# Edge-count products of a graph network on one core: four-pass fp32 against a one-pass format with split operands

## The chip, the core and the metric

The kernel runs on one NeuronCore of one Trainium2 chip. The metric is the device time of one execution in microseconds; several executions are taken and the median counts. Three runs of the kernel before took 2294.43, 2296.43 and 2296.47 us, a median of 2296.43 us.

The engines are called as the profile calls them: PE is TensorE, which multiplies matrices (PEld is its weight load), DVE is VectorE, ACT is ScalarE, POOL is GpSimd, and SP is SyncE, which issues most of the large DMAs. PE writes to PSUM only; DVE and ACT move its results on to SBUF.

## What is computed

The reference runs two blocks of a graph transformer over 625 nodes of 1024 features and 10000 edges. The change lies in the second block's graph part, a two-layer mean-aggregating network, which stands between a linear attention and an attention with experts:

```python
xn = _layernorm(x)
deg_inv = 1 / maximum(segment_sum(ones, dst), 1)
def layer(h, W_self, W_neigh, b):
    agg = segment_sum(h[src], dst)          # sum over incoming edges
    return h @ W_self + (agg * deg_inv[:, None]) @ W_neigh + b
h = relu(layer(xn, W_self0, W_neigh0, b0))
x = x + layer(h, W_self1, W_neigh1, b1) + linear_attention(xn) @ Wo.T + bo
```

With a matrix C whose entry (src, dst) is the number of edges from src to dst, the aggregation is a product: C transposed times h. The kernel builds C once, from one-hot vectors of the edges, and uses it as the operand `CT`.

## The kernel before, in words

The 625 nodes are cut into five tiles (`NT = 5`) of 125 rows (`P`), and the 1024 features into eight chunks (`KC`) of 128 or two column halves of 512. Arrays that end in `T` have features on partitions and nodes along the row, padded to 626 columns (`NP`), which a product takes in two halves of 313 (`HN`). Weights stream from HBM through a pool of six buffers of 1 MB (`wpool`); a `Half` is one column half of a weight matrix and takes two of them. SP issues their DMAs in program order, each when its buffer is free.

In the part from the first edge to the second block's attention, PE, DVE, ACT, POOL and SP run in exactly the order in which the code is written (a hand-made schedule). A small class `Stream` (`do`) arranges it: each call `do(prep, pe, after, after2)` first emits the evictions (`after`) that earlier calls left over, and then its own matmuls (`pe`). So the eviction of a product stands behind whatever DVE work the code wrote between the two calls.

What the change and the steps of the prediction touch, in the order in which it runs:

- `count` and `decode` (L413, L434) build `CT`, an fp32 tile of shape 125 x 5 x 626, for the first block's attention. It then holds integers.
- `degrees` (L985) takes the self loops out of `CT`, multiplies it with a matrix of ones (`pdeg`), and inverts the sums: `dinv`, one number for each column, the same on all partitions. L1010 and L1011 then multiply `CT` by `dinv`, while PE computes keys and values of the linear attention.
- The linear attention's last loop runs over eight chunks `m`. `query(m+1)` computes `pq`, from which ACT makes `qe` and `qf` (L305, L307) and DVE finishes `qf` (L308). `answer(m)` computes `pd` and `po`, and DVE makes `z` and the result `oT` (L324, L325, L326). `qe` and `z` share one buffer; `pq`, `pd` and `po` take turns in three PSUM buffers of two banks (`ps2`). For `m` = 0 and 1, DVE also writes `xnh` (L1025) here, the normalised rows of one column half, five tiles of 125 x 512 each. It stands behind `answer(m)`'s matmuls and ahead of its eviction.
- `pa` (L1039): for each of the eight chunks, `xnh` times `CT`, ten matmuls of 313 columns, copied alternately by DVE and ACT to `meanT`.
- `ph`: the first layer's two weight products, ending in `hT`.
- `pz`: `hT` times `W_neigh1`, copied to `z`, for both column halves, one after the other.
- `last_of(t, c)` (L1125): for tile `t` and column half `c` one PSUM group of 8 matmuls of `hT` with `W_self1`, 8 of `oT` with `Wo` and 5 of `CT` with `z`, each of 512 columns; DVE adds the sum to `x` (L1134). The loop takes `c` = 0 and 1 of a tile, one after the other, with `norm_rows(t-1)` (row statistics on DVE and ACT) between them and `turn_rows(t-1)` (eight transposes `ptr` of the normalised rows and two DVE evictions into `nxT`, L1086) behind them. `px` and `ptr` share two one-bank PSUM buffers (`ps1`).
- `keys`, `q0` and `value` begin the next attention from `nxT`; the first, `keys[0](0)`, reads its columns 0 to 312, so tiles 0 to 2.

Of the kernel before, what the change touches and what calls it, by code (L numbers as in the profile page):

```python
# [8 lines left out]
FP = mybir.dt.float32  # L9
BF = mybir.dt.bfloat16  # L10
HF = mybir.dt.float16
I32 = mybir.dt.int32
AF = mybir.ActivationFunctionType
ALU = mybir.AluOpType
# [4 lines left out]
N = 625  # L19
NT = 5  # L20
# [18 lines left out]


def gps_kernel(tc: tile.TileContext, w: dict, out: bass.AP):


    again = attempt(tc, w, out, False)
    with tc.If(again > 0):
        attempt(tc, w, out, True)
# [3 lines left out]
def attempt(ctx: ExitStack, tc: tile.TileContext, w: dict, out: bass.AP, shifted: bool):  # L50
# [8 lines left out]
    def ps1(name):  # L59
        pool, n = psums[-1]  # L60
        return pool.tile([128, 512], FP, tag="ps1", name=name, bufs=n)
# [33 lines left out]
    def copy(dst, src):  # L95

        turn[0] ^= 1
        if turn[0]:
            nc.vector.tensor_copy(dst, src)
        else:  # L100
            nc.scalar.activation(dst, src, AF.Copy)  # L101
# [21 lines left out]
    def group(dst, pairs):  # L123

        for i, (lhsT, rhs) in enumerate(pairs):
            nc.tensor.matmul(dst, lhsT=lhsT, rhs=rhs, start=(i == 0), stop=(i == len(pairs) - 1))  # L126

    def feat(name, pairs):

        p = ps2(name)  # L130
        for h in range(2):
            group(p[:, h, :HN], [(a, b[:, h * HN:(h + 1) * HN]) for a, b in pairs])
        return p[:, :, :HN]

    def halves(ap):
        return ap.rearrange("p (h n) -> p h n", h=2)

    def nodes(t):
        return slice(t * P, (t + 1) * P)
# [23 lines left out]

    graph = ctx.enter_context(ExitStack())
    gpool = graph.enter_context(tc.tile_pool(name="graph", bufs=1))
    CT = gpool.tile([P, NT, NP], FP, tag="CT", name="CT")
    xrows = w["x"].rearrange("(t p) d -> t p d", p=P)

    class Stream:
# [35 lines left out]
    def mid(shape, name):  # L205
        return midp.tile(shape, FP, tag="mid", name=name)
# [124 lines left out]
    with ExitStack() as st0:  # L331
# [9 lines left out]
        with ExitStack() as edges:  # L341
# [71 lines left out]
            def count():  # L413

                if part["held"] or part["done"] == EN:
                    return False
                lo, hi, t = counting[part["done"]]
                part["held"] = 2 * (t == hi - 1)

                def prep():  # L420
                    while len(made_ahead) < min(8, EN - t):
                        one_hot()
                    hold["hot"] = made_ahead.pop(0)
                    part["done"] += 1

                def pe():
                    od, os = hold["hot"]
                    if t == lo:
                        part["pc"] = psums[-1][0].tile([128, NT, 512], FP, tag="pct", name="pct", bufs=1)
                    for j in range(NT):  # L430
                        nc.tensor.matmul(part["pc"][:P, j, :HN], lhsT=os[:, nodes(j)],
                                         rhs=od[:, :HN], start=(t == lo), stop=(t == hi - 1))

                def decode():  # L434
                    for j in range(0, NT, 2):
                        js = slice(j, min(j + 2, NT))
                        n = js.stop - j
                        low, high, v = CT[:, js, 0:HN], CT[:, js, HN:NP], part["pc"][:P, js, :HN]
                        u = pool.tile([P, 2, HN], FP, tag="u", name="u", bufs=1)[:, 0:n, :]

                        nc.vector.tensor_scalar(u, v, 1728.0, BIG, op0=ALU.subtract, op1=ALU.add)
                        nc.vector.tensor_scalar(u, u, BIG, None, op0=ALU.subtract)
                        if lo == 0:
                            nc.vector.tensor_tensor(low, v, u, op=ALU.subtract)
                            nc.vector.tensor_scalar(high, u, 1.0 / 4096, None, op0=ALU.mult)
                        else:
                            nc.vector.scalar_tensor_tensor(high, u, 1.0 / 4096, high, op0=ALU.mult, op1=ALU.add)
                            nc.vector.tensor_tensor(u, v, u, op=ALU.subtract)
                            nc.vector.tensor_tensor(low, low, u, op=ALU.add)
                    if hi == EN:  # L450

                        for s in range(NT):
                            nc.vector.tensor_tensor(CT[:, s, nodes(s)], CT[:, s, nodes(s)], ident[:P, :P],
                                                    op=ALU.add)

                do(prep, pe, decode if t == hi - 1 else None)
                return True
# [519 lines left out]
        do.flush()  # L977

    dinv = mix.tile([P, NP], FP, tag="qe", name="dinv", bufs=1)
    b0_t = mix.tile([128, KC], FP, tag="bq", name="b0_t", bufs=2)
    nc.gpsimd.dma_start(out=b0_t, in_=w["b0"])

    def degrees():  # L985
        for t in range(NT):
            nc.vector.tensor_tensor(CT[:, t, nodes(t)], CT[:, t, nodes(t)], ident[:P, :P], op=ALU.subtract)

        def pe():
            pdeg = hold["pdeg"] = ps2("pdeg")  # L990
            for h in range(2):
                group(pdeg[:P, h, :HN], [(ones[:P, :P], CT[:, s, h * HN:(h + 1) * HN]) for s in range(NT)])

        def after():
            nc.vector.tensor_scalar(halves(dinv), hold["pdeg"][:P, :, :HN], 1.0, None, op0=ALU.max)
            nc.vector.reciprocal(dinv, dinv)

        do(None, pe, after)

    states = [lin1.states()]  # L1000
    lin1.half(1)
# [5 lines left out]
    for t in range(1, NT):  # L1007
        lin1.key(t)
        lin1.value(t)
        nc.vector.tensor_tensor(CT[:, t, :], CT[:, t, :], dinv, op=ALU.mult)  # L1010
    nc.vector.tensor_tensor(CT[:, 0, :], CT[:, 0, :], dinv, op=ALU.mult)  # L1011
    oT = bigT("oT1")
    lin1.query(0)
    for f in lin1.states():
# [2 lines left out]
    for m in range(KC):  # L1017
        if m + 1 < KC:
            lin1.query(m + 1)
        lin1.answer(m, oT)  # L1020
        if m < 2:

            xh = mid([P, NT, 512], "xnh")
            for t in range(NT):
                nc.vector.tensor_scalar(xh[:, t, :], x[:, t, m * 512:(m + 1) * 512], mv1[:, t, 0:1],  # L1025
                                        rs1[:, t:t + 1], op0=ALU.subtract, op1=ALU.mult)
            xnh.append(xh)
    for name in ("b1", "L1_bo"):
        b_t = mix.tile([128, D], FP, tag="kv", name="b_t", bufs=2)
        nc.gpsimd.dma_start(out=b_t, in_=w[name].to_broadcast([128, D]))  # L1030
# [3 lines left out]
    for k in range(KC):  # L1034
        if k % 4 == 0:
            meanT.append(mid([128, 4, NP], "meanT"))

        def pe():
            hold["pa"] = feat("pa", [(xnh[k // 4][:, s, k % 4 * 128:k % 4 * 128 + 128], CT[:, s, :])  # L1039
                                     for s in range(NT)])  # L1040

        def after(k=k):
            copy(halves(meanT[k // 4][:, k % 4, :]), hold["pa"])

        do(None, pe, after)
    hT = []
    for m in range(KC):
# [10 lines left out]
            nc.scalar.activation(halves(hT[m // 4][:, m % 4, :]), hold["ph"], AF.Relu, bias=b0_t[:, m:m + 1])  # L1058

        do(None, pe, after)  # L1060
    z = big.tile([P, NT, D], FP, tag="big", name="z")
    for c in range(2):
        wn1 = Half(wpool, w["W_neigh1"], c)
        for t in range(NT):
            def pe():
                hold["pz"] = ps1("pz")
                group(hold["pz"][:P], [(hT[k // 4][:, k % 4, nodes(t)], wn1(k)) for k in range(KC)])

            def after(t=t, c=c):
                copy(z[:, t, c * 512:(c + 1) * 512], hold["pz"][:P])  # L1070

            do(None, pe, after)
    ws = [Half(wpool, w["W_self1"], c) for c in range(2)]
    wo = [Half(wpool, w["L1_Wo"], 0), Half(midp, w["L1_Wo"], 1, tag="mid", padded=[128, 4, 645])]
    mixed_up.close()


    rows_d = dram.tile([N + 1, D], FP, name="rows_d")
    y_d = dram.tile([128 * NB, D], FP, name="y_d")
    few = ctx.enter_context(tc.tile_pool(name="few", bufs=1, reuse_waits="tile"))  # L1080
    attn = ctx.enter_context(ExitStack())
    pool = attn.enter_context(tc.tile_pool(name="attn", bufs=1, reuse_waits="tile"))

# [40 lines left out]

    def last_of(t, c):  # L1125
        def pe():
            hold["px"] = ps1("px3")
            group(hold["px"][:P], [(hT[k // 4][:, k % 4, nodes(t)], ws[c](k)) for k in range(KC)]
                  + [(oT[:, k, nodes(t)], wo[c](k)) for k in range(KC)]
                  + [(CT[:, s, nodes(t)], z[:, s, c * 512:(c + 1) * 512]) for s in range(NT)])  # L1130

        def after():
            xc = x[:, t, c * 512:(c + 1) * 512]
            nc.vector.tensor_tensor(xc, hold["px"][:P], xc, op=ALU.add)  # L1134

        do(None, pe, after)

    for t in range(NT):
        last_of(t, 0)
        if t:  # L1140
            norm_rows(t - 1)
        last_of(t, 1)
        if t:
            turn_rows(nxT, t - 1, 0)


    kvc = mid([128, 2 * NP + NT * 256], "kvc")
# [36 lines left out]
                      kcT[:, a, :]) for a in range(2)]  # L1184
    q0 = [query(0, a) for a in range(2)]
    keys[0](0)
    norm_rows(NT - 1)
    keys[1](0)
    q0[0](0)
# [515 lines left out]
```

## Time and profile before

| | us |
|---|---|
| median of three runs | 2296.43 |
| the profiled execution's own time | 2290.41 |
| its span, first to last instruction | 2288.7 |
| POOL's L1032, ten additions to x beside the answers' loop | 24.4 |
| DVE's two copies of `z` and `meanT` (L99), x5 and x4 | 3.5, 3.2 |
| ACT's two copies of `z` and `meanT` (L101), x5 and x4 | 3.0, 2.8 |
| DVE's `CT` by `dinv` (L1010, L1011), x5 | 4.0 |
| `pdeg`, x20 | 5.4 |

The page gives for each group of instructions the line, engine and operation, the tile written and those read, the shapes, the count, the busy time, the mean nanoseconds of one, and the idle time of the engine ahead of it with what ended it. The busy time of a group is the union of its intervals. A PE record is longer than the pace of the instructions, since matmuls overlap: the pace is read from start to start. Each fp32 matmul of the code appears as two MATMUL records with a weight load each: the 80 products of `pa` in the code are x160 in the profile, the 50 products of `CT` with `z` are x100. A bf16 matmul appears once.

The mean granted clock of TensorE over the span is 0.978 of full speed.

### The profile page before, as it was taken

How to read it: one execution, taken by the hardware profiler on the slowest of the kernel's cores; microseconds unless marked ns; L12 is line 12 of the kernel's file. 1: busy time of each engine (PE TensorE's matmuls, PEld its weight loads, DVE VectorE, ACT ScalarE, POOL GpSimd, SP SyncE). 2: the span in 40 equal slices, each digit the busy share in tenths (PEclk: the TensorE clock that was granted, in tenths of full speed). 3: DMA queues.
4: the chain of work that ended last, by engine and by line, in shares of the span. 5: the costliest groups of instructions: out<-in, count | busy, mean ns of one | idle time of the engine just before them, and what ended most of it. 6: DMA issues, size and time to landing. Idle time of an engine off the chain costs nothing. (4 is left out here: it accounts for less than half of the span.)

```text
span 2288.7 us, 17693 instructions
## 1 busy us (share of the span) xinstructions
PE 2170.3 (95%) x7018; PEld 1228.9 (54%) x7018; DVE 734.7 (32%) x1342; ACT 196.1 (9%) x363; POOL 346.0 (15%) x351
## 2 busy tenths in 40 slices
PE   8988888987899999999999999999999999999998
PEld 6655554444445767754444777556754444444443
DVE  5868668655422640000111133232111111111112
ACT  2000010012200100000000011110000000000000
POOL 1667766300000220010000000010000000000010
PEclk9998998989999999999999999999999999999999
DMA  9352252530122110233003111030269898898643
GB/s 302 96 174 63 68 186 79 133 105 1 37 83 74 46 46 0 74 138 110 0 0 118 57 38 37 10 109 1 92 249 338 318 332 305 303 332 319 254 149 94
DMA packets 145852, 301.66 MB, mean 132 GB/s; under 512 B 12370, under 2 KB 22436, under 8 KB 145754
## 3 DMA queue, kind: packets, MB, share of 16 engines
q1 hardware_dynamic: 123412, 243.18, 29.6%
q0 software_dynamic: 17664, 47.47, 7.0%
q10 hardware_dynamic: 4678, 9.72, 1.4%
q8 instruction: 59, 0.97, 0.2%
q14 instruction: 39, 0.32, 0.0%
HBM read 277.49 MB, written 22.84 MB: 131 GB/s over the span
## 5 line engine op out<-in xcount | busy, mean ns | idle before, releaser
L126 PE MATMUL pu<-w,xgT 128*128 128x512 f32 x768 | 333.9, 593 | 1.9 <-DVE xgT L1086 1.9
L126 PEld LDWEIGHTS pu<-w,xgT 128*128 128x128 f32 x768 | 144.0, 190 | 174.8 <-issue 172.0
L126 PE MATMUL pyb<-w,hb 128*128 128x512 f32 x384 | 174.3, 598 | 2.5 <-ACT yb L101 2.1
L126 PE MATMUL pq<-xnT,w 128*128 128x313 f32 x512 | 143.0, 439 | 15.1 <-ACT qf L307 11.6
L126 PE MATMUL pv<-w,xnT 128*125 128x512 f32 x320 | 143.4, 602 | 3.7 <-issue 3.7
L126 PE MATMUL pk<-w,xnT 128*125 128x512 f32 x320 | 141.4, 595 | 4.7 <-DVE x L888 4.7
L126 PE MATMUL p<-tT,w 128*128 128x313 f32 x512 | 136.3, 428 | 0.4 <-DVE tT L1086 0.4
L126 PEld LDWEIGHTS pq<-xnT,w 128*128 128x128 f32 x512 | 99.6, 196 | 56.9 <-ACT qf L307 13.5
L126 PEld LDWEIGHTS pyb<-w,hb 128*128 128x128 f32 x384 | 69.8, 189 | 90.9 <-issue 74.9
L1539 DVE TENSOR_TENSOR su<-pu,su 128x512 f32<-128x512 f32 x24 | 16.6, 691 | 314.6 <-ACT su L1538 314.6
L126 PEld LDWEIGHTS p<-tT,w 128*128 128x128 f32 x512 | 96.8, 190 | 37.9 <-issue 1.2
L126 PEld LDWEIGHTS pk<-w,xnT 128*125 128x125 f32 x320 | 59.7, 189 | 78.9 <-issue 72.2
L126 PEld LDWEIGHTS pv<-w,xnT 128*125 128x125 f32 x320 | 60.4, 191 | 76.7 <-issue 75.9
L582 POOL DMA_INDIRECT table<-es,at x79 | 85.9, 1088 | 59.9 <-issue 27.2
L1522 POOL DMA_INDIRECT xg<-rows_d,slots x12 | 11.4, 947 | 524.7 <-PE pxg L1529 449.0
L568 POOL DMA_INDIRECT ga<-xl_d,si x79 | 81.1, 1027 | 32.1 <-issue 29.1
L568 POOL DMA_INDIRECT gb<-xr_d,di x79 | 79.6, 1008 | 24.1 <-issue 23.5
L706 PE MATMUL px<-w,oT 128*125 128x512 f32 x160 | 76.7, 639 | 4.1 <-DVE oT L326 2.3
L126 PE MATMUL px<-w,hT 128*125 128x512 f32 x160 | 70.6, 594 | 0.0
L126 PE MATMUL px<-w,oT 128*125 128x512 f32 x160 | 70.3, 592 | 0.0
L126 PE MATMUL ph<-meanT,w 128*128 128x313 f32 x256 | 70.1, 426 | 0.0
L126 PE MATMUL ph<-xnT,w 128*128 128x313 f32 x256 | 70.0, 427 | 0.0
(352 smaller groups left out, 2550.9 us busy)
## 6 DMA issues: line engine op xcount, KB each, us to landing
w<-in_eW_dram SPq DMA_DIRECT2D x144, 1024.0 KB
w<-in_L_Wk_dram SPq DMA_DIRECT2D x8, 1024.0 KB
w<-in_L_Wv_dram SPq DMA_DIRECT2D x8, 1024.0 KB
w<-in_L_Wq_dram SPq DMA_DIRECT2D x8, 1024.0 KB
w<-in_L_Wo_dram SPq DMA_DIRECT2D x8, 1024.0 KB
w<-in_W_self_dram SPq DMA_DIRECT2D x8, 1024.0 KB
w<-in_W_neigh_dram SPq DMA_DIRECT2D x8, 1024.0 KB
w<-in_sW_dram SPq DMA_DIRECT2D x8, 1024.0 KB
```

The lines of the kernel that those rows point to most:

```text
L126: nc.tensor.matmul(dst, lhsT=lhsT, rhs=rhs, start=(i == 0), stop=(i == len(pairs) - 1))
L568: nc.gpsimd.indirect_dma_start(out=dst[0:p, j, :], out_offset=None, in_=src[:, :], in_offset=bass.IndirectOffsetOnAxis(ap=ix[0:p, lo + j:l ...
L582: nc.gpsimd.indirect_dma_start(out=table[:, :], out_offset=bass.IndirectOffsetOnAxis(ap=at[0:p, lo + j:lo + j + 1], axis=0), in_=es[0:p, l ...
L706: nc.tensor.matmul(hold["px", t][:P, c, :], lhsT=oT[:, k, nodes(t)], rhs=wo[c](k), start=(k == 0), stop=False)
L1522: nc.gpsimd.indirect_dma_start(out=xg, out_offset=None, in_=rows_d[:, :], in_offset=bass.IndirectOffsetOnAxis(ap=slots[:, b:b + 1], axis=0))
L1539: nc.vector.tensor_tensor(su, pu[:, 0, :], su, op=ALU.mult)
```

## The change

`CT` becomes a tile of the type float32r (`FR`), a 4-byte format of reduced precision that TensorE is to take in one pass; its whole edge counts are written in it. Where other code reads it, it is seen as fp32 through a bitcast. `CT` is no longer multiplied by `dinv`; the degrees are applied to the results instead. The other operand of each product, which isn't made of small integers, is split into a high part (an ACT copy rounded to the format) and a low part (DVE: the value less the high part), and both are multiplied with `CT` into the same sum. The last products are taken by column halves: all five tiles of the first half, then `z` and the weights of the second half, then its tiles. (The path `shifted` is a second attempt with full fp32 and isn't run for these inputs.)

```diff
-    CT = gpool.tile([P, NT, NP], FP, tag="CT", name="CT")
+    CTr = gpool.tile([P, NT, NP], FP if shifted else FR, tag="CT", name="CT")
+    CT = CTr if shifted else CTr.bitcast(FP)
...
     def degrees():
...
         def after():
-            nc.vector.tensor_scalar(halves(dinv), hold["pdeg"][:P, :, :HN], 1.0, None, op0=ALU.max)
+            nc.vector.tensor_scalar(halves(dinv), hold["pdeg"][:, :, :HN], 1.0, None, op0=ALU.max)
+            if not shifted:
+                most = sage.tile([128, 1], FP, name="most")
+                nc.vector.tensor_reduce(most, dinv, AX.X, ALU.max)
+                nc.vector.tensor_scalar(inside[:, 1:2], most, 4095.0, None, op0=ALU.is_le)
             nc.vector.reciprocal(dinv, dinv)
+            own = mix.tile([P, NP], FP, tag="qe", name="own", bufs=1)[:, 0:N].rearrange("p (t n) -> p t n", t=NT)
+            nc.vector.tensor_tensor(own, dinv[:P, 0:N].rearrange("p (t n) -> p t n", t=NT),
+                                    ident[:P, :P].unsqueeze(1).to_broadcast([P, NT, P]), op=ALU.mult)
+            nc.vector.tensor_reduce(dinvT, own, AX.X, ALU.add)
...
+    def split(src, high, low):
+        nc.scalar.activation(high, src, AF.Copy)
+        if not shifted:
+            nc.vector.tensor_tensor(low, src, high.bitcast(FP), op=ALU.subtract)
...
     for t in range(1, NT):
         lin1.key(t)
         lin1.value(t)
-        nc.vector.tensor_tensor(CT[:, t, :], CT[:, t, :], dinv, op=ALU.mult)
-    nc.vector.tensor_tensor(CT[:, 0, :], CT[:, 0, :], dinv, op=ALU.mult)
...
         lin1.answer(m, oT)
         if m < 2:
-            xh = mid([P, NT, 512], "xnh")
+            parts = [midp.tile([P, NT, 512], NUM, tag="mid", name="xnh")]
+            parts.append(sage.tile([P, NT, 512], NUM, name="xnl") if m else
+                         midp.tile([P, NT, 512], NUM, tag="mid", name="xnl"))
             for t in range(NT):
-                nc.vector.tensor_scalar(xh[:, t, :], x[:, t, m * 512:(m + 1) * 512], mv1[:, t, 0:1],
+                xh = mix.tile([P, 512], FP, tag=("kb", "ke")[t % 2], name="xh", bufs=1)
+                nc.vector.tensor_scalar(xh, x[:, t, m * 512:(m + 1) * 512], mv1[:, t, 0:1],
                                         rs1[:, t:t + 1], op0=ALU.subtract, op1=ALU.mult)
-            xnh.append(xh)
+                split(xh, parts[0][:, t, :], parts[1][:, t, :])
+            xnh.append(parts[0:1] if shifted else parts)
...
         def pe():
-            hold["pa"] = feat("pa", [(xnh[k // 4][:, s, k % 4 * 128:k % 4 * 128 + 128], CT[:, s, :])
-                                     for s in range(NT)])
+            p = hold["pa"] = ps2("pa")
+            for h in range(2):
+                group(p[:, h, 0:HN + 1], [(xp[:, s, k % 4 * 128:k % 4 * 128 + 128],
+                                           CTr[:, s, h * (HN - 1):h * (HN - 1) + HN + 1])
+                                          for xp in xnh[k // 4] for s in range(NT)])
 
         def after(k=k):
-            copy(halves(meanT[k // 4][:, k % 4, :]), hold["pa"])
+            m = meanT[k // 4][:, k % 4, :]
+            for h in range(2):
+                nc.vector.tensor_tensor(m[:, h * HN:(h + 1) * HN], hold["pa"][:, h, h:h + HN],
+                                        dinv[:, h * HN:(h + 1) * HN], op=ALU.mult)
...
-    z = big.tile([P, NT, D], FP, tag="big", name="z")
-    for c in range(2):
+    z, ws, wo = [], [], []
+    def neighbours(c):
+        zc = big.tile([P, 2, NT, 512], NUM, tag="big", name="z")
+        z.append(zc)
         wn1 = Half(wpool, w["W_neigh1"], c)
+        ws.append(Half(wpool, w["W_self1"], c))
+        wo.append(Half(wpool, w["L1_Wo"], c))
         for t in range(NT):
...
-            def after(t=t, c=c):
-                copy(z[:, t, c * 512:(c + 1) * 512], hold["pz"][:P])
+            def after(t=t):
+                split(hold["pz"][:P], zc[:, 0, t, :], zc[:, 1, t, :])
...
-    ws = [Half(wpool, w["W_self1"], c) for c in range(2)]
-    wo = [Half(wpool, w["L1_Wo"], 0), Half(midp, w["L1_Wo"], 1, tag="mid", padded=[128, 4, 645])]
+    neighbours(0)
...
     def last_of(t, c):
         def pe():
-            hold["px"] = ps1("px3")
-            group(hold["px"][:P], [(hT[k // 4][:, k % 4, nodes(t)], ws[c](k)) for k in range(KC)]
-                  + [(oT[:, k, nodes(t)], wo[c](k)) for k in range(KC)]
-                  + [(CT[:, s, nodes(t)], z[:, s, c * 512:(c + 1) * 512]) for s in range(NT)])
+            p = hold["px"] = ps2("px3")
+            group(p[:P, 0, :], [(hT[k // 4][:, k % 4, nodes(t)], ws[c](k)) for k in range(KC)]
+                  + [(oT[:, k, nodes(t)], wo[c](k)) for k in range(KC)])
+            group(p[:P, 1, :], [(CTr[:, s, nodes(t)], z[c][:, i, s, :]) for i in range(1 if shifted else 2)
+                                for s in range(NT)])
 
         def after():
             xc = x[:, t, c * 512:(c + 1) * 512]
-            nc.vector.tensor_tensor(xc, hold["px"][:P], xc, op=ALU.add)
+            nc.vector.tensor_tensor(xc, hold["px"][:P, 0, :], xc, op=ALU.add)
+            nc.vector.scalar_tensor_tensor(xc, hold["px"][:P, 1, :], dinvT[:, t:t + 1], xc,
+                                           op0=ALU.mult, op1=ALU.add)
...
     for t in range(NT):
         last_of(t, 0)
+    neighbours(1)
+    for t in range(NT):
+        last_of(t, 1)
         if t:
             norm_rows(t - 1)
-        last_of(t, 1)
-        if t:
-            turn_rows(nxT, t - 1, 0)
+        if t > 1:
+            turn_rows(nxT, t - 2, 0)
...
     keys[0](0)
+    turn_rows(nxT, NT - 2, 0)
     norm_rows(NT - 1)
```

The small pool `few` moves to the other end of SBUF; `pdeg` has 128 instead of 125 stationary columns; `dinvT` is a column of five inverse degrees for each partition.

More of the change, by code (lines that the diff above doesn't have):

```diff
@@ L11 @@
 HF = mybir.dt.float16
+FR = mybir.dt.float32r
 I32 = mybir.dt.int32
@@ L438, in decode @@
                         low, high, v = CT[:, js, 0:HN], CT[:, js, HN:NP], part["pc"][:P, js, :HN]
+                        low_r, high_r = CTr[:, js, 0:HN], CTr[:, js, HN:NP]
                         u = pool.tile([P, 2, HN], FP, tag="u", name="u", bufs=1)[:, 0:n, :]
@@ L443, in decode @@
                         if lo == 0:
-                            nc.vector.tensor_tensor(low, v, u, op=ALU.subtract)
-                            nc.vector.tensor_scalar(high, u, 1.0 / 4096, None, op0=ALU.mult)
+                            nc.vector.tensor_tensor(low_r, v, u, op=ALU.subtract)
+                            nc.vector.tensor_scalar(high_r, u, 1.0 / 4096, None, op0=ALU.mult)
                         else:
-                            nc.vector.scalar_tensor_tensor(high, u, 1.0 / 4096, high, op0=ALU.mult, op1=ALU.add)
+                            nc.vector.scalar_tensor_tensor(high_r, u, 1.0 / 4096, high, op0=ALU.mult, op1=ALU.add)
                             nc.vector.tensor_tensor(u, v, u, op=ALU.subtract)
-                            nc.vector.tensor_tensor(low, low, u, op=ALU.add)
+                            nc.vector.tensor_tensor(low_r, low, u, op=ALU.add)
                     if hi == EN:
                         for s in range(NT):
-                            nc.vector.tensor_tensor(CT[:, s, nodes(s)], CT[:, s, nodes(s)], ident[:P, :P],
+                            nc.vector.tensor_tensor(CTr[:, s, nodes(s)], CT[:, s, nodes(s)], ident[:P, :P],
                                                     op=ALU.add)
@@ L977, in attempt @@
         do.flush()
-    dinv = mix.tile([P, NP], FP, tag="qe", name="dinv", bufs=1)
+    few = ctx.enter_context(tc.tile_pool(name="few", bufs=1, side="right", reuse_waits="tile"))
+    sage = mixed_up.enter_context(tc.tile_pool(name="sage", bufs=1, reuse_waits="tile"))
+    dinv = sage.tile([128, NP], FP, name="dinv")
+    dinvT = few.tile([P, NT], FP, name="dinvT")
     b0_t = mix.tile([128, KC], FP, tag="bq", name="b0_t", bufs=2)
@@ L986, in degrees @@
         for t in range(NT):
-            nc.vector.tensor_tensor(CT[:, t, nodes(t)], CT[:, t, nodes(t)], ident[:P, :P], op=ALU.subtract)
+            nc.vector.tensor_tensor(CTr[:, t, nodes(t)], CT[:, t, nodes(t)], ident[:P, :P], op=ALU.subtract)
         def pe():
@@ L991, in pe @@
             for h in range(2):
-                group(pdeg[:P, h, :HN], [(ones[:P, :P], CT[:, s, h * HN:(h + 1) * HN]) for s in range(NT)])
+                group(pdeg[:, h, :HN], [(ones[:P, :], CT[:, s, h * HN:(h + 1) * HN]) for s in range(NT)])
         def after():
-            nc.vector.tensor_scalar(halves(dinv), hold["pdeg"][:P, :, :HN], 1.0, None, op0=ALU.max)
+            nc.vector.tensor_scalar(halves(dinv), hold["pdeg"][:, :, :HN], 1.0, None, op0=ALU.max)
[3 more added lines that the diff above has]
+                nc.vector.tensor_scalar(inside[:, 1:2], most, 4095.0, None, op0=ALU.is_le)
             nc.vector.reciprocal(dinv, dinv)
+            own = mix.tile([P, NP], FP, tag="qe", name="own", bufs=1)[:, 0:N].rearrange("p (t n) -> p t n", t=NT)
+            nc.vector.tensor_tensor(own, dinv[:P, 0:N].rearrange("p (t n) -> p t n", t=NT),
+                                    ident[:P, :P].unsqueeze(1).to_broadcast([P, NT, P]), op=ALU.mult)
+            nc.vector.tensor_reduce(dinvT, own, AX.X, ALU.add)
         do(None, pe, after)
+    def split(src, high, low):
+        nc.scalar.activation(high, src, AF.Copy)
+        if not shifted:
+            nc.vector.tensor_tensor(low, src, high.bitcast(FP), op=ALU.subtract)
+    NUM = FP if shifted else FR
     states = [lin1.states()]
@@ L1079, in attempt @@
     y_d = dram.tile([128 * NB, D], FP, name="y_d")
-    few = ctx.enter_context(tc.tile_pool(name="few", bufs=1, reuse_waits="tile"))
     attn = ctx.enter_context(ExitStack())
```

## The prediction

> **What bounds the kernel now.** The chain of waits is of no use here: it breaks off 77 us before the end. So I read the busy times first, then stretches of the span around the change, then groups by shape, then the timeline.
>
> ```profile
> PE 2170.3 (95%) x7018; PEld 1228.9 (54%) x7018; DVE 734.7 (32%) x1342; ACT 196.1 (9%) x363; POOL 346.0 (15%) x351
> 720.00:823.20 103.20, 97.19 (x379) 68.42 (x377) 59.20 (x56) 12.91 (x18) 25.51 (x12) 1.00 0.25 90
> 823.20:867.10 43.90, 43.90 (x160) 31.34 (x161) 8.93 (x7) 2.08 (x3) 0.00 (x0) 0.96 0.00 0
> 1070.60:1257.20 186.60, 185.17 (x453) 81.92 (x452) 22.84 (x49) 4.24 (x10) 0.11 (x1) 1.00 0.15 54
> ```
>
> After the stretch and its length come PE, PEld, DVE, ACT and POOL busy, then clock, DMA share and GB/s. PE is the bound, above all in the second (`pa`) and third (`last_of`) stretches, with DVE, ACT and the DMAs far below. A microsecond off PE there is one off the end, as long as nothing is late.
>
> **What the two products cost.** The paces come from start to start:
>
> ```profile
> L126 PE MATMUL px<-z,CT 125*125 125x512 f32 x100 | 44.6, 592 | 0.0
> L126 PE MATMUL pa<-CT,xnh 125*128 125x313 f32 x160 | 44.1, 439 | 3.5 <-DVE oT L326 3.5
> 1251.56 4.46 PE L126 MATMUL px<-z,CT 125*125 125x512 f32 x10
> 1255.86 0.59 PE L151 MATMUL ptr<-ident,xs 125*128 125x125 f32 x4
> 110.24 4.16 PE L431 MATMUL pct<-ring 128*125 128x313 bf16 x30
> 114.24 7.03 PE L126 MATMUL pv<-w,xnT 128*125 128x512 f32 x16
> 476.21 1.03 PE L126 MATMUL pdn<-dn,room 128*125 128x512 bf16 x4
> ```
>
> Ten records of 512 fp32 columns take 4.30 us, 429 ns each. In bf16, 30 records of 313 columns take 4.00 us, 133.3 ns each, and four of 512 take 1.03 us with a last record of 0.38: (1.03 - 0.38)/3 = 217 ns. So an fp32 record costs two bf16 ones and an fp32 product, being two records, four. The change makes two one-pass matmuls of each product: as many records as before, at half the time each. No row shows the 4-byte one-pass format at this size. Its cost lies between the bf16 pace and no gain (429 and 264); I take the bf16 pace, because a pass of fp32 already streams 4-byte columns at it. 314 columns then take 133.5 ns, 512 take 216.
>
> The Trainium skill ("TensorE: Matmul & The Clock Gate", Back-to-back issue gap) gives 131 ns for 512 columns in a real stream, by pipelining. By it the 100 matmuls with `z` would take 13.1 us instead of 21.6, and I would forecast 8.5 us less. Nothing here runs so: the fp32 and the bf16 row agree on some 215 ns a pass. I keep the row.
>
> - `pa`: 43.9 us before. After: 160 x 0.1335 = 21.4, and 2 us because it begins behind an idle PE at half clock (until 827.2 the records of before come every 0.52 us instead of 0.26: 4 us at half pace). **Saved: 20.5.**
> - `CT` with `z`: ten groups of 4.29 = 42.9 before; 100 x 0.216 = 21.6 after. **Saved: 21.3.**
>
> **The answers' loop.** Here the change puts work on a path that is nearly full.
>
> ```profile
> 749.86 1.22 PE L126 MATMUL pd<-qf,kv 128*128 128x313 f32 x4
> 750.91 1.22 PE L126 MATMUL po<-qf,kv 128*128 128x313 f32 x4
> 751.97 8.59 PE L126 MATMUL pq<-xnT,w 128*128 128x313 f32 x32
> 752.28 2.36 DVE L1025 TENSOR_SCALAR xnh<-x,mv,rs 125x512 f32<-125x512 f32 x5
> 754.56 0.80 DVE L324 TENSOR_SCALAR z<-pd 128x626 f32<-128x626 f32 x1
> 755.39 4.07 DVE L325 RECIPROCAL z<-z 128x626 f32<-128x626 f32 x1
> 759.56 0.81 DVE L326 TENSOR_TENSOR oT<-po,z 128x626 f32<-128x626 f32 x1
> 760.64 0.78 ACT L305 ACTIVATE qe<-pq,bq 128x626 f32<-128x626 f32 x1 [9.13 <-PE pq L126]
> 762.51 8.59 PE L126 MATMUL pq<-xnT,w 128*128 128x313 f32 x32
> ```
>
> `oT` ends at 760.37, just ahead of the 760.64 at which `qe` takes over the buffer of `z`. The slack is 0.3 us. In place of 2.28 us for five `xnh`, DVE now does, five times: `xh` 0.54, waits for ACT's copy (0.63, as ACT's L246), then subtracts (0.69, as an SBUF sum of 512 columns), with 0.04 at each hand-over and starts that overlap a little: 1.89 x 5 = 9.4. DVE runs in program order, so the next tile's `xh` can't fill the wait. Queued behind it is the eviction of `pd` and `po`, later by 7.2: `oT` ends at 767.5. Who waits: `pd(1)` for the PSUM that `z` reads (762.5), `po(1)` for that of `oT` (767.5), ACT's `qe` for the buffer, and `pq(3)` for the PSUM that ACT's `qf` reads, 1.5 us on: it starts at 769.1 instead of 762.51, 6.6 late. The second half repeats it with no slack left: 7.0. **Lost: 13.6.**
>
> PE then stands idle twice for 3.9 us between `pd` and `po`. The skill (same page, Part 1) speaks against such gaps: a whole idle window of 3.4 us on a free-running grid halves the clock. Taken literally a gap of 3.9 holds a whole window once in seven, so 0.3 us in the mean. The trace is harsher:
>
> ```profile
> 299.64 11.46 PE L126 MATMUL pq<-xnT,w 128*128 128x313 f32 x32 [4.70 <-ACT qf L307]
> ```
>
> These 32 take 8.59 at full clock, so 2.9 were lost. Gaps of 3.49, 3.73 and 3.91 were followed by losses of 1.2 to 2.7, one of 3.51 by none. I take 2.3 for each, but the first falls into PE's wait for `z` of the second round (2.5 us) and costs nothing: **lost 2.0** to 2.3, I take 2.0.
>
> **The transposes.** Each of four `turn_rows` took 1.42 to 1.54 us from its first transpose to the next product, since `ptr` shared two PSUM buffers with `px`; together 6.0. With `px` elsewhere they run at their own pace (107 ns, from the eight at 1269.93): 4 x 0.86 = 3.4. But `keys[0](0)` now follows tile 2's transposes at once and needs its evictions, behind two additions of the last `px` (0.69; 0.75 as L888): some 1.3 us of wait. **Saved: 1.3.**
>
> **Edits at nothing.** Five multiplications of `CT` (4.0 us) go from DVE and a reduction, a product and a reduction (0.8 each) come; DVE is free between keys and values, PE needing 13.7 us a pair. `pa`'s evictions by `dinv` are all DVE's, two of 313 columns, some 0.48 each by the 256- and 626-column rows (0.42, 0.81); PE needs 2.67 a chunk, and the last is covered by 4.2 us of `ph` that doesn't read it. Were it not, 1 us. The split of `pz` (ACT 0.60, DVE 0.69) lies beside 6.87 us of PE a tile, and its last is read 13.7 us later. SP: the second half's `W_neigh1` loads once the first's two buffers are free, 80 us ahead of its use; `W_self1` and `Wo` load beside the second `pz`, 34 us for 4 MB, 12.7 at the 330 GB/s that later slices reach. `Wq` waits for `W_self1`'s last use, as now. POOL's zeros and memset keep some 120 us of cover.
>
> **Sum.** 20.5 + 21.3 + 1.3 - 13.6 - 2.0 = 27.5 us less. The profiled execution (span 2288.7, own time 2290.4) becomes 2262.9. The median lies 6.0 above that execution, so I forecast 2296.4 - 27.5 = **2269**.
>
> **Rivals.**
> - *The answers' loop swallows the split*: DVE is 57% busy in that stretch, ACT 13%. Against it: 0.3 us of slack, one buffer, fixed order. All gains and no loss: 2296.4 - 43.1 = 2253. Chance 0.2.
> - *Slower: the 4-byte format isn't one pass.* If float32r takes two passes, the products cost what they did (twice the matmuls, half the passes) and the loop's 15.6 remains: 2296.4 - 1.3 + 15.6 = 2311. It decides from the pace at which 14.3 of the 41.8 are left: some 356 ns for 512 columns. For it: no such row. Against it: the pace of an fp32 pass. Chance 0.06.
> - *The weight load isn't hidden.* fp32 loads are longer than bf16 ones (189 against 141 ns) and set a pace of 113 ns where only 65 columns follow (`pg`, 22.7 us x200). Added to each matmul, 247 and 329 ns: saved 2.4 + 10.0, net 2298, no change. Against it: at 313 columns both formats hide it. Chance 0.04.
> - *The loop costs more*: half clock in both rounds, or a slower conversion, up to 12 us more: 2281. Chance 0.15.
>
> The likeliest case has 0.55. The range, 2249 to 2284, takes in the first and last. What can't be told from no change is 0.2%, 4.6 us: faster 0.90, same 0.04, slower 0.06.
>
> **What would show it.** `pa` x160 at some 22 to 24 us busy, `CT` with `z` x100 at 21 to 22; PE idle some 14 us longer in the answers' loop, put down to DVE's `z` or `oT` and ACT's `qf`, with `pq` above 8.6 after it; no 0.36 us gaps in `ptr`, one of 1.3 ahead of `pkc`. I am wrong if `pa` stays near 40, or if the loop keeps its 10.54 us from one `pq` to the next.

## The result and the profile after

The changed kernel takes 2271.45 us (median of four runs, 2268.09 to 2276.30) against 2295.43 for the kernel before (four runs on the same chip): a ratio of 0.9898, with a 95% interval of 0.9876 to 0.992. The forecast was 2269, in a range of 2249 to 2284. The profiled execution took 2268.09 us, its span 2266.3.

The busy times and the two products in the groups by shape:

```profile
PE 2137.9 (94%) x7018; PEld 1226.9 (54%) x7018; DVE 756.3 (33%) x1378; ACT 202.6 (9%) x374; POOL 344.7 (15%) x351
L129 PE MATMUL px<-z,CT 125*125 125x512 f32 x100 | 28.7, 433 | 0.0
L129 PE MATMUL pa<-CT,xnh 125*128 125x314 f32 x80 | 15.9, 333 | 3.5 <-DVE oT L330 3.5
L129 PE MATMUL pa<-CT,xnl 125*128 125x314 f32 x80 | 15.5, 328 | 0.0
```

As many records as before, 100 and 160, and they are shorter. Their busy times overstate them: a record is modelled longer than the pace, so the ends of short groups overlap what follows. The timeline has the pace. First `pa`, from its first record to the first of `ph`:

```profile
840.12 1.67 PE L129 MATMUL pa<-CT,xnh 125*128 125x314 f32 x5 [3.49 <-DVE oT L330]
841.59 1.51 PE L129 MATMUL pa<-CT,xnl 125*128 125x314 f32 x5
...
864.70 0.90 PE L129 MATMUL pa<-CT,xnh 125*128 125x314 f32 x5
865.44 0.90 PE L129 MATMUL pa<-CT,xnl 125*128 125x314 f32 x5
866.18 4.38 PE L129 MATMUL ph<-xnT,w 128*128 128x313 f32 x16
```

It took 26.06 us instead of 43.94. Five records take 0.72 to 0.74 us at full clock, some 146 ns each, and nearly double behind the idle PE at the start. Then one group of the last products:

```profile
1035.37 7.03 PE L129 MATMUL px<-w,hT 128*125 128x512 f32 x16
1042.24 7.03 PE L129 MATMUL px<-w,oT 128*125 128x512 f32 x16
1048.70 2.86 PE L129 MATMUL px<-z,CT 125*125 125x512 f32 x10
1051.40 7.03 PE L129 MATMUL px<-w,hT 128*125 128x512 f32 x16
```

From one `hT` to the next are 16.03 us, of which the two fp32 products take 6.87 each. The ten with `z` are left with 2.29, 229 ns each, instead of 4.29. Their first record is placed 0.4 us early, over the end of the product with `oT`; the other nine have the same pace, 2.06 us from 1049.34 up to the next `hT`. The third piece is the answers' loop, here its first disturbed round:

```profile
753.37 8.59 PE L129 MATMUL pq<-xnT,w 128*128 128x313 f32 x32
753.67 0.54 DVE L1050 TENSOR_SCALAR xh<-x,mv,rs 125x512 f32<-125x512 f32 x1
754.30 0.63 ACT L1018 ACTIVATE xnh<-xh 125x512 fp32r<-125x512 f32 x1 [1.38 <-issue]
755.03 0.69 DVE L1020 TENSOR_TENSOR xnl<-xh,xnh 125x512 fp32r<-125x512 f32 x1 [0.81 <-ACT xnh L1018]
755.64 0.54 DVE L1050 TENSOR_SCALAR xh<-x,mv,rs 125x512 f32<-125x512 f32 x1
...
763.02 0.80 DVE L328 TENSOR_SCALAR z<-pd 128x626 f32<-128x626 f32 x1
763.86 4.07 DVE L329 RECIPROCAL z<-z 128x626 f32<-128x626 f32 x1
763.88 2.31 PE L129 MATMUL pd<-qf,kv 128*128 128x313 f32 x4 [1.92 <-DVE z L328]
768.89 2.45 PE L129 MATMUL po<-qf,kv 128*128 128x313 f32 x4 [2.71 <-DVE oT L330]
768.96 0.78 ACT L309 ACTIVATE qe<-pq,bq 128x626 f32<-128x626 f32 x1 [6.58 <-DVE oT L330]
771.14 10.17 PE L129 MATMUL pq<-xnT,w 128*128 128x313 f32 x32
```

The splits keep DVE from 753.67 to 763.02, with 0.7 to 0.8 us of waiting for ACT in each. `pd` waits for `z`, `po` and ACT's `qe` for `oT`, and the next `pq` starts 17.77 us after the last one instead of 10.54 and runs partly at half clock (10.17 instead of 8.59). The last piece is the wait ahead of the keys, behind the transposes of tile 2:

```profile
1231.86 1.01 PE L154 MATMUL ptr<-ident,xs 125*128 125x125 f32 x8
1234.17 4.48 PE L129 MATMUL pkc<-nxT,wkc 128*128 128x313 f32 x16 [1.30 <-DVE nxT L1124]
```

The account of the two profiled executions, in us (negative is time saved):

| step | forecast | measured | from |
|---|---|---|---|
| `pa` | -20.5 | -17.9 | 43.94 to 26.06 |
| `CT` with `z` | -21.3 | -20.0 | ten groups, 4.29 to 2.29 |
| answers' loop, clock included | +15.6 | +15.5 | second to sixth `pq`, 42.15 to 57.67 |
| transposes and the keys' wait | -1.3 | -1.2 | 6.03 to 3 x 0.85 + 2.31 |
| ahead of the second `pq` | 0 | +1.4 | 741.43 to 742.83 |
| sum | -27.5 | -22.2 | own times: 2290.41 to 2268.09, -22.3 |

In six profiles of kernels with the changed kernel's code ahead of this loop, on chips on which the kernel before took some 2295 us, its first query began between 727.3 and 737.8 us. So the 1.4 us are within what executions differ by.

### The profile page after: what moved, and what is told of

It is laid out like the page before. It is cut to its first block, busy times and chain, and to the rows that moved or that the text cites. A ratio compares the mean times of both kernels' runs of the same rounds, so it can differ in the third digit from the quotient of the medians.

```text
span 2266.3 us, 17746 instructions
## 1 busy us (share of the span) xinstructions
PE 2137.9 (94%) x7018; PEld 1226.9 (54%) x7018; DVE 756.3 (33%) x1378; ACT 202.6 (9%) x374; POOL 344.7 (15%) x351
## 5 line engine op out<-in xcount | busy, mean ns | idle before, releaser
L1020 DVE TENSOR_TENSOR z<-pz,z 125x512 fp32r<-125x512 f32 x10 | 6.9, 690 | 196.8 <-ACT z L1018 196.8
```

Of the source, the lines that this page charges most:

```text
L1020: nc.vector.tensor_tensor(low, src, high.bitcast(FP), op=ALU.subtract)
```

## The experiments

The theory was that the two products bring some 40 us, and that the splits for `pa` give 15 of them back because of where they stand on DVE: evictions that PE needs are queued behind work that waits for ACT. The rivals: DVE's added work costs that wherever it stands, or only the half clock does. The first four ran on a chip on which the kernel before took 2347.8 us and the part ahead of the loop some 50 us longer, so they are read by ratios and stretches.

**The splits spread over five answers.**

```diff
     for m in range(KC):
         if m + 1 < KC:
             lin1.query(m + 1)
+        low_parts()
         lin1.answer(m, oT)
-        if m < 2:
...
+        for c, t in todo[2 * m:2 * m + 2]:
+            half_rows(c, t)
```

`half_rows` issues `xh` and ACT's copy of one of the ten tiles, `low_parts` the subtractions that the answer before left over.

> The ten row tiles are split two for each of the answers m = 0 to 4, and each subtraction is moved behind the next eviction of pd and po, so that DVE no longer waits for ACT's copy; the work is the same. If the loss in the answers' loop is the order on DVE (evictions queued behind splits and their waits), pq starts every 10.54 us again, seven queries take what they took before (42.2 us from the second pq to the sixth, instead of 57.7), and the median falls by some 15.5 from 2271.5 to about 2256. Rival, that the 12 us of added DVE work costs wherever it stands in this loop: 2268 to 2271. Rival, that only the half clock behind the two gaps costs: some 3 us less, 2268.

The timeline of PE, the queries alone:

```profile
799.02 8.59 PE L129 MATMUL pq<-xnT,w 128*128 128x313 f32 x32
...
809.56 8.59 PE L129 MATMUL pq<-xnT,w 128*128 128x313 f32 x32
...
820.10 8.59 PE L129 MATMUL pq<-xnT,w 128*128 128x313 f32 x32
...
830.64 8.59 PE L129 MATMUL pq<-xnT,w 128*128 128x313 f32 x32
...
841.18 8.59 PE L129 MATMUL pq<-xnT,w 128*128 128x313 f32 x32
...
862.78 8.69 PE L129 MATMUL pq<-xnT,w 128*128 128x313 f32 x32 [0.25 <-ACT qf L311]
```

From the second to the sixth query are 42.16 us, 10.54 each: all of the loss in these periods is gone with the same work on DVE and ACT. The spread work reaches one answer further; from the second to the eighth query, the last, are 63.76 us, 0.5 more than the 63.23 before. The ratio to before was 0.9839 (0.9808 to 0.987). Both rivals fall.

**The splits by kind, at their old place.** Five `xh`, five copies, five subtractions, with the five `xh` in one larger buffer (`plain`).

> The splits stay where they are, but by kind: five normalisations, five ACT copies, five subtractions. DVE does the same work (some 5.7 us a half) without the hand-over waits (9.4). If the waits are about half of the loss, each half delays the evictions by 3.4 instead of 7.2: 6.5 us lost for both instead of 13.6, and 2 to 3 for the half clock, since po still stands 3.9 behind pd: median about 2264. Rival, that DVE's work alone makes the loss: no change, 2271. Rival, that the clock alone does: 2271, with the pq after each gap still at 10 us.

```profile
811.81 2.37 DVE L1050 TENSOR_SCALAR plain<-x,mv,rs 125x512 f32<-125x512 f32 x5
814.09 3.09 DVE L1056 TENSOR_TENSOR xnl<-plain,xnh 125x512 fp32r<-125x512 f32 x5
817.10 0.80 DVE L328 TENSOR_SCALAR z<-pd 128x626 f32<-128x626 f32 x1
...
819.92 1.22 PE L129 MATMUL pd<-qf,kv 128*128 128x313 f32 x4
822.97 1.32 PE L129 MATMUL po<-qf,kv 128*128 128x313 f32 x4 [1.83 <-DVE oT L330]
824.54 8.69 PE L129 MATMUL pq<-xnT,w 128*128 128x313 f32 x32 [0.25 <-ACT qf L311]
```

DVE needs 5.3 us a half here (811.81 to 817.10), and `z` is done in time for `pd`. The four periods take 47.67 us, 5.5 more than undisturbed. Of the 15.5 lost in the changed kernel, DVE's work at this place in its order is 5.5; 10 are the hand-over waits and the slower clock that came with them. The expected 2 to 3 us for the clock didn't come: with gaps of 1.83 and 2.12 us the queries behind them ran at full pace (8.69 and 8.70 us), at a granted clock of 1.00. Ratio 0.9855 (0.9827 to 0.9883).

**Only the last products in one pass**, `pa` in fp32.

> Only the last products take the one-pass format; pa multiplies fp32 rows by the edge counts in fp32, as before, and the degrees are still applied to its results. The loop then holds the five normalisations of before. If the loop's loss belongs to the split for pa, it goes (15.5) and pa goes back from 26.1 to 43.9 us (17.8): median about 2274, so the conversion of pa is worth 2 to 3 us net as it stands. Rival, that the loss came with something else (the degrees, memory taken by other tiles): the loss stays and pa is 18 us longer: 2289.

```profile
884.55 42.41 PE L129 MATMUL pa<-CT,xnh 125*128 125x313 f32 x160 [3.49 <-DVE oT L330]
926.81 4.38 PE L129 MATMUL ph<-xnT,w 128*128 128x313 f32 x16
```

The loop took 42.15 us and `pa` 42.26, at a granted clock of 1.00 from its start. So in these two stretches converting `pa` as the change does brings almost nothing here: without it 15.7 us come back in the loop and 16.1 are lost in `pa`, against the next experiment's profile, which has both splits. The ratio, 0.9933 (0.9899 to 0.9967), was worse than that, and the first query began 10 us later than in the next one with the same code ahead of it; the 10 us arose in the first block, between 403 and 435 us. It was run again, below.

**Half the stationary columns in the last products**: `CTr[:, s, t * P:t * P + 64]` instead of 125 columns.

> The last products load 64 instead of 125 stationary columns, so the second layer's neighbour sum is left out for rows 64 to 124 of each tile. A float32r matmul of 512 columns took 229 ns, 13 more than a bf16 one. If an uncovered part of the 4-byte weight load is the 13 ns, it shrinks with half the columns: 216 to 222 ns, the ten in a group 2.2 us instead of 2.29. If the format has a fixed cost for each matmul, 229 stays. Either way the total moves by less than 1.5 us.

```profile
L129 PEld LDWEIGHTS px<-z,CT 125*64 125x64 f32 x100 | 13.5, 135 | 13.0 <-issue 5.3
1085.77 7.03 PE L129 MATMUL px<-w,hT 128*125 128x512 f32 x16
...
1101.84 7.03 PE L129 MATMUL px<-w,hT 128*125 128x512 f32 x16
```

The weight load fell from 186 to 135 ns, and the period stayed, 16.07 us against 16.03. So in the products with `z` the 13 ns don't follow the length of the load. In `pa`, whose load records (some 190 ns at full clock) are longer than the pace, this wasn't tried. The one run took 2318.76 us, and the changed kernel wasn't run on this chip, so its total says nothing.

**The changed kernel again, and bf16 parts.** From here on the kernel before took about 2294 us.

> The changed kernel itself, so that the next three stand beside it on one chip. From the second to the sixth pq some 57.7 us, pa 26, ten matmuls with z 2.29 a group.

The four periods took 57.67 us, `pa` 26.10; the median was 2269.84, the ratio 0.9891 (0.9876 to 0.9906).

```diff
-    NUM = FP if shifted else FR
+    NUM = FP if shifted else BF
...
+        CTb = whole_pool.tile([P, NT, NP], BF, name="CTb")
...
-                                           CTr[:, s, h * (HN - 1):h * (HN - 1) + HN + 1])
+                                           CTb[:, s, h * (HN - 1):h * (HN - 1) + HN + 1])
```

> The same splits and the same places, but the high and low parts and a copy of the edge counts are bf16 instead of float32r (five ACT copies more, beside keys and values[...]). If the 13 ns over the bf16 pace are a fixed cost of the float32r format, they go: 133.5 ns for 314 columns and 216 for 512, pa at full clock 1.33 for ten instead of 1.46, a group with z 2.16 instead of 2.29, together 3.3 us less than the changed kernel. If they come from something that both have (two groups open in two PSUM banks, the two parts), nothing changes.

```profile
868.17 0.83 PE L129 MATMUL pa<-CTb,xnh 125*128 125x314 bf16 x5
868.84 0.83 PE L129 MATMUL pa<-CTb,xnl 125*128 125x314 bf16 x5
869.51 4.38 PE L129 MATMUL ph<-xnT,w 128*128 128x313 f32 x16
...
1052.43 2.32 PE L129 MATMUL px<-z,CTb 125*125 125x512 bf16 x10
1054.59 7.03 PE L129 MATMUL px<-w,hT 128*125 128x512 f32 x16
```

Five records take 0.667 us, 133.3 ns each, and a group with `z` 2.16. So the surcharge goes with the format: 13 ns for each float32r matmul, whether it streams 314 columns or 512. `pa` is 3.4 us shorter than in the changed kernel's second profile, 2.1 of it by the pace and 1.3 because less of its start fell at half clock; the stretch from the first `px` to the keys is 1.5 shorter. Yet the median, 2269.69, is that of the changed kernel. In the profiles the first query began 3.0 us later here (735.83 against 732.80), with no more added ahead of it than five ACT copies beside PE work, and first queries of kernels that are the same up to there differ by more. Medians of four runs that spread over 4 or 5 us don't part gains of this size.

**The tail filled.** On top of the spread splits, two `pa` go ahead of the last answer, where PE waited for `qf` (2.0 us) and for PSUM (3.49). `neighbour_mean(k)` is the code of `pa` for chunk `k`.

```diff
+        if m == KC - 1:
+            neighbour_mean(0)
+            neighbour_mean(1)
         lin1.answer(m, oT)
...
+    for k in range(2, KC):
+        neighbour_mean(k)
```

> The spread splits, and in addition the first two pa are issued ahead of the last answer, where PE waited 2.0 us for qf and 3.5 for PSUM. If these gaps and the half clock behind them (pa took 26.1 us, 160 x 0.146 would be 23.4) are what the tail costs, PE stands idle there 2 us instead of 5.5 and pa loses little to the clock: 15.5 by the spread and 5 to 6 by the filling, some 21 us less than the changed kernel. Rival, that the last answer only moves behind pa and its chain on DVE ends later by as much: 15.5 less, as the spread alone.

```profile
807.14 8.70 PE L129 MATMUL pq<-xnT,w 128*128 128x313 f32 x32
...
817.55 1.12 PE L129 MATMUL pa<-CT,xnh 125*128 125x314 f32 x5
...
824.21 1.32 PE L129 MATMUL pd<-qf,kv 128*128 128x313 f32 x4 [0.46 <-DVE oT L330]
...
843.95 4.38 PE L129 MATMUL ph<-xnT,w 128*128 128x313 f32 x16
```

From the last query to `ph` are 36.81 us (807.14 to 843.95) instead of 44.49 in the changed kernel's second profile: 7.7 less, more than expected, since the gap is 0.46 and `pa` runs at full clock throughout (granted 1.00 from 817.5 to 844). Median 2247.45, ratio 0.9795 (0.9777 to 0.9814).

**The transposes one tile earlier.** `turn_rows(nxT, t - 2, 0)` is moved ahead of `last_of(t, 1)`.

> As the one with the filled tail, and the transposes of tile t - 2 stand ahead of the last products of tile t instead of behind them. The 1.3 us of wait ahead of the first keys goes: some 22 us less than the changed kernel, a ratio to before of about 0.980.

```profile
1213.90 2.88 PE L129 MATMUL px<-z,CT 125*125 125x512 f32 x10
1216.62 4.38 PE L129 MATMUL pkc<-nxT,wkc 128*128 128x313 f32 x16
```

The keys follow the products without a wait. Median 2245.77 (2243.44 to 2250.48), ratio 0.9792 (0.9776 to 0.9808): 24 us below the changed kernel beside it and 49 below the kernel before. This is the best version found; that it beats the one before it rests on the stretch alone, the medians don't part them.

**Two of the first four again**, on a chip on which the kernel before took 2294.29.

> The spread splits once more, because the first four experiments ran on a chip on which the part ahead of the loop took some 50 us longer and differed by up to 10 us from kernel to kernel. By the stretches (42.2 us instead of 57.7 for the four periods) its total should lie 15.5 below the changed kernel: a ratio to before of about 0.983.

The four periods took 42.15 us. Median 2255.14, ratio 0.9828 (0.9806 to 0.9849).

> Only the last products in the one-pass format, once more, for the same reason. By the stretches the loop gives back 15.5 and pa costs 16 to 18 more, so its total should lie 0 to 3 us above the changed kernel: a ratio to before of 0.989 to 0.991. If it stays near the 0.9933 of the first chip, something ahead of the loop differs between the two kernels that the stretches don't show.

The four periods took 42.15 us and `pa` 43.94, part of it at half clock this time. Median 2271.04, ratio 0.9909 (0.989 to 0.9928). So the extra loss of the first chip didn't come back. What lengthened the part ahead of the loop there stays open. Its four traces have two things that no other has: `pct`, the products that build `CT`, wait 26 to 33 us for nothing that the profile names, and the mean clock of the first 700 us is 0.89 to 0.91 instead of 0.93 or 0.94. Converting `pa` as the change does it, splits and all, brings 0.4 us in the stretches on the first chip and 2.4 by this profile and the changed kernel's, and nothing that the medians show (ratios 0.9898 and 0.9891 with it, 0.9909 without); with the splits spread it is worth some 16 us (2255.14 against 2271.04).

## Why the prediction was right

**Two passes instead of four: right.** The records were as many as before at about half the time; no two-pass float32r. The term that was off is the pace. The forecast took the bf16 pace, 133.5 and 216 ns, "because a pass of fp32 already streams 4-byte columns at it". It was 146 and 229. That is 2.0 us in `pa` and 1.3 with `z`. The bf16 variant shows it to be a cost of the format for each matmul, the same at 314 and at 512 moving columns, and the half load shows that at 512 it doesn't depend on the stationary ones. Which part of the format's handling it is, no run shows. Half an fp32 record, 215 ns of 429, is short of it by 14, so the argument from that pace missed it.

**The skill's 131 ns for 512 columns** ("TensorE: Matmul & The Clock Gate", Back-to-back issue gap): nothing ran at it, neither float32r (229) nor bf16 (216). Keeping the row was right.

**The answers' loop: right, in place, waiters and size.** 15.5 against 15.6; in the three disturbed periods 7.2, 6.9 and 1.4 where 6.6, 7.0 and 2.0 were worked out. The splits took 9.35 us where 9.4 was worked out. That the loss comes from where the work stands and from the hand-over, not from the amount of work, is shown by the spread splits, and the shares by the batched ones.

**The clock: right in the loop, too small in `pa`.** Stretches of the changed kernel, with the columns of the prediction's stretches (the granted clock is the third number from the end), and the end of the second disturbed round:

```profile
753.40:764.00 10.60, 8.68 (x34) 5.98 (x33) 6.97 (x13) 3.15 (x5) 0.00 (x0) 1.00 0.00 0
764.10:774.30 10.20, 7.49 (x15) 4.35 (x15) 7.06 (x6) 2.72 (x4) 0.00 (x0) 0.50 0.00 0
784.60:791.30 6.70, 4.98 (x10) 3.31 (x11) 4.85 (x5) 1.46 (x2) 0.00 (x0) 0.50 0.28 101
839.20:845.90 6.70, 5.78 (x22) 5.78 (x23) 6.40 (x4) 0.00 (x0) 0.00 (x0) 0.50 0.00 0
...
787.07 0.78 ACT L311 ACTIVATE qf<-pq,bq 128x626 f32<-128x626 f32 x1
788.57 9.98 PE L129 MATMUL pq<-xnT,w 128*128 128x313 f32 x32
```

In the loop PE stood idle for 8.3 us (1.92, 2.71 and 3.69), not for the 14 that were named as a sign, and worked 12.5 at half clock. Most of the slow work cost nothing, because DVE's chain ended later: the slow query of the first round (10.17 us) was done just as `z` was, as forecast. ACT's `qf` of the second round ends at 787.85; a query starting there would make the loss by order 13.4 us (34.48 from the query at 753.37, less two periods of 10.54), where 13.6 was forecast. It started at 788.57, behind a `po` at half clock, and took 9.98 us instead of 8.59: together 2.1 for the clock, where 2.0 was forecast (an estimate from these rows and those of `pq`, `po` and `qf`).

The skill's rule on idle gaps (same page, Part 1), taken literally, gave 0.3 us in the mean. The trace doesn't agree with it: at 764.1 the clock was halved already, behind an idle stretch of 1.92 us, shorter than the rule's 3.4, and so it was in the changed kernel's second profile. The length of a gap alone doesn't decide it either, since 1.83 and 2.12 us in the batched run cost no clock; what does is not shown here.

`pa`'s start cost 2.7 us (26.06 less 160 x 0.1462), not 2.0. The same gap of 3.49 us stands ahead of `pa` in ten profiles and cost from nothing to 2.8 us, so that 2.0 came near is luck in part.

**The transposes and the keys' wait: right**, 1.30 for 1.3.

**The rivals.** "The loop swallows the split" was wrong as the change stood, and would have been right with two tiles per answer: its argument, that DVE and ACT have time, holds over the stretch and fails in the order. Of "the loop costs more", the half clock in both rounds did happen, but it was hidden behind DVE in the first and the up to 12 us didn't come. Two passes for float32r and an exposed weight load (247 and 329 ns by its sum) didn't happen.

**The sum** was 5.2 too large against the profile (3.3 from the pace, 0.7 from the clock in `pa`, 1.4 from ahead of the loop, with rounding) and 3.5 against the medians (27.5 and 24.0).

## What to carry to other kernels

When work is added to an engine that runs in program order, don't ask whether the engine has time but what is queued behind the addition and how much slack that has: with 0.3 us of slack, evictions that came 7 us later made the kernel 7 us longer, twice, and two tiles at a time, with each subtraction behind the next eviction, gave it all back. A hand-over to another engine and back inside such a queue costs the wait as well; issue the parts by kind (5.5 us lost instead of 15.5), or pick the result up one round later (none in the same periods). And price a format by a record of that format: half an fp32 record and a float32r matmul differ by 14 ns, little in one, over 3 us in 260.

## What the hardware showed unexpectedly

Start to start, a float32r matmul took 146 ns for 314 moving columns and 229 for 512, a bf16 one in its place 133 and 216: 13 ns more at both lengths. Halving the stationary columns shortened the load by 51 ns without moving the pace of 512. Ahead of `pa` the same gap of 3.49 us was followed by 5.9 us at half clock in the changed kernel, by some 3.4 in the kernel before and by none in one run, while in the loop 1.92 us was followed by half clock and 1.83 and 2.12 us weren't. On one of the chips the same code took some 50 us longer ahead of the loop and differed by up to 10 us between kernels, while the loop and the float32r `pa` agreed with the other chips to 0.2 us.
